# Bias rows and norm vectors of a graph network: operands filled up with zeros to 128 rows and columns

## The chip, the cores and the metric

The kernel runs on one core of one Trainium2 chip. The metric is the device time of one execution in microseconds (us). Names of the engines in the views: PE is TensorE's matmul, PEld its weight load, DVE is VectorE, ACT is ScalarE, POOL is GpSimd, SP is SyncE, which here only issues transfers. A matmul's stationary operand is called its weights; "granted clock" is the share of TensorE's full clock.

## The reference

There are 32 independent batches of a graph with 512 nodes, 128 features each, and an adjacency matrix of zeros and ones. Four graph layers follow each other, each on relu(layernorm(x)) and with a residual addition. All four are needed to place the change; the change itself is in the second (layer 1):

```python
x = x + max over neighbours of relu(p_i + q_j + b)          # layer 0
x = x + L1(relu(layernorm(x)), adj)                         # layer 1
x = x + (adj / rowsum(adj)) @ (h @ weight) + bias           # layer 2
x = x + four GRU steps with messages adj.T @ (h @ W)        # layer 3

# L1: four inner layers; nodes are the concatenated earlier outputs
src_agg = l2norm(adj, rows)      @ (nodes @ ws + bs)
dst_agg = l2norm(adj, columns).T @ (nodes @ wd + bd)
out     = tanh(concat(src_agg, nodes @ wn + bn, dst_agg) @ wu + bu)
```

The bias of the aggregated terms, bs and bd, reaches a node weighted by the sum of its normalised adjacency row or column. With zeros and ones this sum is the square root of the degree.

## The kernel before

**Weights.** `FastWeights` prepares what all batches share. Its constructor makes an identity, index codes and other constants directly, before the planner runs. `rest` folds ws, wn and wd of layer 1 with wu into the weights `w1`, and folds bs and bd with wu into eight rows per inner layer: `b8`, a tile of [8, 4, 128] in fp32r (a form of f32 that TensorE reads in one pass). Eight rows are needed because the weights and the degree vectors are each kept in a high and a low part for precision.

**One batch** goes through `prepare`, `gathers`, `layer1` and `layer23`.

- `prepare` loads x and the adjacency, forms the first layernorm (xn), the transposed adjacency (at, through pat) and the degrees (deg). Then it forms six vectors of norms, `sc`, a tile of [128, 6, 4] f32: GpSimd takes the power -1/2 of the degrees (two vectors), multiplies by the degree (g), rounds that to fp32r (g1, copied into sc) and subtracts (the last write into sc). `dinv` is the square of the first vector. One transposition on TensorE, `psc`, turns the 24 columns of sc into 24 rows, ScalarE copies them (sct), and SP writes them to a table in device memory, `scals`. The key matmuls (pkey) and the maximum over them (top, row, idx) stand around this in time.
- `gathers` computes layer 0: indirect transfers (G) bring most neighbours' rows, one-hot matmuls (pa, from oh and qhl) the others, and VectorE takes the maximum (gm, acc).
- `layer1` reads the table back, once as broadcast scales (rbc) and twice as rows (row8, 8 rows of 512). ScalarE rounds row8 into `rows`, [8, 512] fp32r. For each of the four inner layers it aggregates (pg, from hi and lo against at and an), and forms the output in one accumulator, `pu`: first the bias rows' matmul of b8 and rows, 8 rows high, and then the f32 matmuls with w1 over the features (hT, f) and aggregates (ag). A tanh on ScalarE makes f.
- `layer23` does layers 2 and 3 (pg, po, ph, pk, phn, pxn, gates, zc, nn, h).

An f32 matmul over 512 columns is recorded as two instructions, an fp32r one as one.

**The order of the work** is not written out. `Flow` is a planner in the kernel: operations are noted with an estimated cost (`cost`, `mm`, `tr`), their dependencies follow from tiles and regions, and a list scheduler (`step`) issues them engine by engine, by due times with hand-set leads (`LEADS`). Up to six parts are open at a time, so parts of several batches interleave on every engine. A matmul's cost is taken from its moving columns and type alone, not from its rows. Where the planner foresees TensorE idle, it puts in `spin` matmuls without use (line 534). Nearly all operations carry the line of the planner's call, L510, so the views are read by tile names.

Buffers: tiles with a `tag` come from rings of `bufs` places; `rows` has one place, `sc` four.

```python
self.note("pe", self.nc.tensor.matmul, (out, lhsT, rhs), {"start": start, "stop": stop},
          [group or out], [lhsT, rhs], cost, 0.16)
```

Of the kernel before, what the change touches and what calls it, by code (L numbers as in the profile page):

```python
# [13 lines left out]
F32 = mybir.dt.float32  # L14
F32R = mybir.dt.float32r
# [4 lines left out]
ALU = mybir.AluOpType  # L20
# [4 lines left out]
P = 128  # L25
# [35 lines left out]
NL1 = 4  # L61
# [4 lines left out]
def flat(t):  # L66
    return t.rearrange("p t d -> p (t d)")
# [217 lines left out]
class Flow:  # L285
# [46 lines left out]
    def fixed(self, t, shape, dtype):  # L332

        return View(Buf(None, 0, shape[0], t), shape, dtype)
# [269 lines left out]
class FastWeights:  # L604
# [5 lines left out]
    def __init__(self, nc, F, a, const, mid, ps):  # L610
        self.F, self.mid, self.ps = F, mid, ps
        self.NL3 = a["L3_gnn_weight"].shape[0]
        n = a["x"].shape[1]

        def fixed(shape, dtype, name):
            return const.tile(shape, dtype, name=name)

        ident = fixed([P, P], F32, "ident")
        make_identity(nc, ident)
        identb = fixed([P, P], BF16, "identb")  # L620
        nc.vector.tensor_copy(identb, ident)
        self.ident, self.identb = ident, identb
        self.mhalf = fixed([P, 8], F32, "mhalf")
        nc.gpsimd.memset(self.mhalf, -0.5)

        self.ones = fixed([P, P], F32, "ones")
        nc.gpsimd.memset(self.ones, 1.0)  # L630
        ltf = fixed([P, P], F32, "ltf")
        nc.gpsimd.affine_select(
            ltf, self.ones, pattern=[[1, P]], compare_op=ALU.is_ge, fill=0.0, base=0,
            channel_multiplier=-1,
        )
        nc.gpsimd.memset(ltf[0:HP, HP:P], 0.0)
        self.lt = fixed([P, P], F32R, "lt")
        nc.vector.scalar_tensor_tensor(self.lt, ident, NBASE, ltf, ALU.mult, ALU.add)
        self.ltk = fixed([P, P], BF16, "ltk")
        nc.vector.tensor_scalar(self.ltk, self.lt.bitcast(F32), KEY, None, ALU.mult)  # L640
        self.code = fixed([P, n // P, P], BF16, "code")
        icode, code = fixed([P, n // P], I32, "icode"), fixed([P, n // P], F32, "fcode")
        for t, (first, step) in enumerate(CODES):
            nc.gpsimd.iota(
                icode[:, t : t + 1], pattern=[[1, 1]], base=first, channel_multiplier=step
            )
        nc.vector.tensor_copy(code, icode)
        for t in range(n // P):
            nc.vector.tensor_scalar(
                self.code[:, t, :], ident, code[:, t : t + 1], None, ALU.mult  # L650
            )


        self.sign = fixed([P, 2], F32, "sign")
        nc.gpsimd.memset(self.sign[:, 0:1], -1.0)
        nc.gpsimd.memset(self.sign[:, 1:2], 1.0)
        nc.gpsimd.memset(self.sign[0:4, 0:1], 1.0)
        nc.gpsimd.memset(self.sign[0:4, 1:2], 0.0)
        self.nc, self.a, self.const, self.n = nc, a, const, n

    def own(self, shape, dtype, name):
        return self.F.tile(self.const, shape, dtype, name, name)

    def temp(self, tag, name, wide=False):
        shape = [P, 2, self.n] if wide else [P, 4, P]
# [26 lines left out]
    def rest(self):  # L692

        F, a, ident, NL3 = self.F, self.a, self.ident, self.NL3

        n3 = 3 * NL3
        brow = self.temp("zc", "brow")[:, 0, :]
        F.pool.memset(brow, 0.0)
        rows = [
            ((nm, i), a[f"L1_gnn_{nm}{i}"].unsqueeze(0), 1)  # L700
            for i in range(NL1) for nm in ("bs", "bd", "bn", "bu")
        ] + [
            (nm, a[f"L3_gnn_b_{nm}"].rearrange("l (g c) -> (l g) c", c=P), n3)
            for nm in ("ih", "hh")
        ]
        col, at = {}, 0
        for key, src, m in rows:
            col[key] = at
            (F.sync, F.act)[len(col) % 2].dma_start(out=brow[at : at + m, :], in_=src)
            at += m  # L710
        pb = self.psum("pb")
        F.tr(pb[:, 0, :], brow, ident)
        bcol = self.own([P, P], F32, "bcol")
        F.vec.tensor_copy(bcol, pb[:, 0, :])
        self.bih = bcol[:, col["ih"] : col["ih"] + n3]
        self.bhh = bcol[:, col["hh"] : col["hh"] + n3]
        self.bsum = self.own([P, n3], F32, "bsum")
        F.vec.tensor_add(self.bsum, self.bih, self.bhh)

        self.w1, self.bu = [], self.own([P, NL1], F32, "bu")

        self.b8 = self.own([8, NL1, P], F32R, "b8r")
        bm = self.own([P, NL1, 2, 8], F32, "bm")
        F.pool.memset(bm, 0.0)
        for i in range(NL1):
            for k, nm in enumerate(("bs", "bd")):
                c = col[nm, i]
                F.act.copy(bm[:, i, k, k::2], bcol[:, c : c + 1].to_broadcast([P, 4]))  # L730
        for i in range(NL1):
            ch = NCH[i]
            wu = self.temp("x2", f"wu{i}")[:, 0:3, :]
            F.sync.dma_start(out=wu, in_=a[f"L1_gnn_wu{i}"].rearrange("(c p) v -> p c v", p=P))
            w1 = self.own([P, 3, ch, P], F32, f"w1_{i}")
            for k, nm in enumerate(("ws", "wn", "wd")):
                w = self.temp(("f", "hg", "hT1")[k], f"{nm}{i}")[:, 0:ch, :]
                (F.sync, F.act)[k % 2].dma_start(
                    out=w, in_=a[f"L1_gnn_{nm}{i}"].rearrange("(c p) v -> p c v", p=P)
                )  # L740
                pt = self.psum(f"pwt_{i}_{k}")
                for c in range(ch):
                    F.tr(pt[:, c, :], w[:, c, :], ident)
                wt = self.temp(("gate0", "xn2")[k % 2], f"wt_{i}_{k}")[:, 0:ch, :]
                F.vec.tensor_copy(wt, pt[:, 0:ch, :])
                pw = self.psum(f"pw_{i}_{k}")
                for c in range(ch):
                    F.mm(pw[:, c, :], wt[:, c, :], wu[:, k, :], start=True, stop=True)
                F.act.copy(w1[:, k, :, :], pw[:, 0:ch, :])
            self.w1.append(w1)  # L750
            pv = self.psum(f"pv_{i}")
            c = col["bn", i]
            F.mm(
                pv[:, 2, 0:1], wu[:, 1, :], bcol[:, c : c + 1], start=True, stop=True, group=pv
            )
            for k in range(2):
                F.mm(
                    pv[0:8, 0, :], bm[:, i, k, :], wu[:, 2 * k, :],
                    start=(k == 0), stop=(k == 1), group=pv,
                )  # L760
            c = col["bu", i]
            F.vec.tensor_add(self.bu[:, i : i + 1], bcol[:, c : c + 1], pv[:, 2, 0:1])
            hi = F.tile(self.mid, [P, 4, P], F32R, "hi1", f"bhi_{i}", 1)[0:8, 0, :]
            F.act.copy(hi, pv[0:8, 0, :])
            full = self.temp("nn", f"bfull_{i}")[0:8, 0, :]
            F.vec.tensor_scalar(full, pv[0:8, 0, :], self.sign[0:8, 1:2], None, ALU.mult)
            F.vec.scalar_tensor_tensor(
                self.b8[:, i, :], hi.bitcast(F32), self.sign[0:8, 0:1], full, ALU.mult, ALU.add
            )

    def last(self):
# [51 lines left out]
def fast(ctx: ExitStack, tc: tile.TileContext, a: dict, out: bass.AP, bad):  # L823
    nc = tc.nc
    x, adj, nodemask = a["x"], a["adj"], a["nodemask"]
    B, N, D = x.shape
    assert D == P and N % P == 0
    NT = N // P

    const = ctx.enter_context(tc.tile_pool(name="const", bufs=1))  # L830
    small = ctx.enter_context(tc.tile_pool(name="small", bufs=3))
# [3 lines left out]
    F = Flow(nc, PACE, AHEAD)  # L835
# [9 lines left out]
    mid = ctx.enter_context(tc.tile_pool(name="mid", bufs=1))  # L845
    W = FastWeights(nc, F, a, const, mid, ps)
# [6 lines left out]
    for i in range(2):  # L853
        t = dram.tile([ROWS, P], F32, name=f"qtab{i}")
        k = (ROWS - 2 * P) // P
# [75 lines left out]
    def prepare(b, xt, af):  # L931
# [83 lines left out]

        dm = F.tile(small, [P, 2, NT], F32, tag="dm", name=f"dm_{b}", bufs=4)
        F.pool.tensor_scalar(dm, deg, 1.0, None, ALU.max)
        sc = F.tile(small, [P, 6, NT], F32, tag="sc", name=f"sc_{b}", bufs=4)
        F.pool.tensor_tensor(
            sc[:, 0:2, :], dm, W.mhalf[:, 0 : 2 * NT].rearrange("p (k t) -> p k t", k=2), ALU.pow  # L1020
        )
# [30 lines left out]
        F.vec.tensor_scalar(idx, row[:, :, 0:NLEFT], ROWS - 1, None, ALU.bitwise_and)  # L1052

        pt = pst(0, f"psc_{b}")
        F.tr(pt[0 : 6 * NT, 0, :], sc.rearrange("p k t -> p (k t)"), W.ident)
        sct = F.tile(small, [6 * NT, P], F32, tag="sct", name=f"sct_{b}", bufs=1)
        F.act.copy(sct, pt[0 : 6 * NT, 0, :])
        F.sync.dma_start(out=scals[b % 2].rearrange("k (t p) -> (k t) p", p=P), in_=sct)
# [49 lines left out]
    def layer1(b, x1, an, at, dinv):  # L1108
# [3 lines left out]
            F.sync.dma_start(out=row8[4 * h : 4 * h + 4, :], in_=scal[2:6, :])  # L1112
        rbc = F.tile(mid, [P, 2, N], F32, tag="rbc", name=f"rbc_{b}")
        F.sync.dma_start(out=rbc, in_=scal[0:2, :].unsqueeze(0).to_broadcast([P, 2, N]))
        rows = F.tile(mid, [8, N], F32R, tag="rows", name=f"rows_{b}")

        xn = norm(1, x1, f"{b}_1")
        two = sbuf_parts(1, xn, f"{b}_1")
        F.act.copy(rows, row8)
        pt = transposed(1, xn, f"pt_{b}_1")  # L1120
        hT = F.tile(mid, [P, NT, P], F32, tag="hT1", name=f"hT_{b}_1")
        F.act.copy(hT, pt)
# [3 lines left out]
        for i in range(NL1):  # L1126
# [10 lines left out]
                F.vec.tensor_mul(ag[:, k, :], flat(pg), rbc[:, k, :])  # L1137
            agg[new] = ag
            pu = pst(1, f"pu_{b}_{i}")
            F.mm(flat(pu), W.b8[:, i, :], rows, start=True, stop=False)  # L1140
            late = []
            for c, nm in enumerate(names):
                F.mm(flat(pu), w[:, 1, c, :], flat(feat[nm]), start=False, stop=False)
# [626 lines left out]
```

## Time and profile before

| | |
|---|---|
| median of 3 runs | 2941.53 us (2940.82 to 2942.3) |
| profiled execution | 2943.54 us, span 2941.8 us |
| mean granted TensorE clock | 0.993 |
| busy, TensorE matmul | 2843.4 us (97% of the span), 11493 records |
| busy, VectorE | 2384.2 us (81%) |
| busy, GpSimd | 1827.3 us (62%) |
| busy, ScalarE | 1218.1 us (41%) |
| bias rows' matmuls | 128 |
| transpositions psc | 32 |

The span runs from the first to the last instruction of one profiled execution; its own time is a little longer. Busy times are unions of an engine's instructions. Matmuls are pipelined, so their records overlap, and the rate of TensorE is read from the distances between their starts.

A matmul's form in the views reads rows*columns of the weights, then partitions x elements of what is written or read: "8*128 8x512" is a matmul with 8 rows of weights, 128 columns, and 512 moving columns; "128*24 128x128" is the transposition of 24 columns. "x4" in a timeline means four records in a row.

### The profile page before, as it was taken

What the parts mean: (1) busy time and instruction counts of PE and PEld (TensorE: products, weight loads), DVE (VectorE), ACT (ScalarE), POOL (GpSimd) and SP (SyncE); (2) the same over time, 40 slices, a digit from 0 to 9 for tenths busy, and PEclk for the clock granted to TensorE, in tenths of its full rate; (3) what the DMA queues carried; (4) which work ended last, traced back from release to release, by engine and by line L of the source; (5) the groups of instructions that cost most, each with busy time, mean ns of one, the idle gap of its engine ahead of it and who ended that gap; (6) DMA issues with size and microseconds to landing.
All of it is one profiled execution on the core that took longest, in us unless ns stands there. A gap on an engine that the chain in (4) does not pass through costs nothing.

```text
span 2941.8 us, 37748 instructions
## 1 busy us (share of the span) xinstructions
PE 2843.4 (97%) x11493; PEld 1753.8 (60%) x11513; DVE 2384.2 (81%) x5382; ACT 1218.1 (41%) x2547; POOL 1827.3 (62%) x2013
## 2 busy tenths in 40 slices
PE   7899999999999999999999999999999999999997
PEld 3555556666666566666666566666666666555555
DVE  6988878888888898888888888889888888887533
ACT  2434434434444344344444444444344444333323
POOL 4676667666666666666666666666666666565312
PEclk8999999999999999999999999999999999999999
DMA  7642434334334334333433433343333333342100
GB/s 154 145 91 48 84 69 86 85 72 81 65 66 86 85 74 86 59 72 80 86 85 73 84 61 65 86 87 77 80 68 69 75 86 84 56 77 37 33 4 9
DMA packets 191267, 218.44 MB, mean 74 GB/s; under 512 B 30376, under 2 KB 139600, under 8 KB 191056
## 3 DMA queue, kind: packets, MB, share of 16 engines
q0 software_dynamic: 47104, 92.34, 22.2%
q1 hardware_dynamic: 73768, 63.63, 7.4%
q10 hardware_dynamic: 70184, 59.98, 6.7%
q8 instruction: 93, 1.52, 0.2%
q14 instruction: 118, 0.97, 0.1%
HBM read 164.32 MB, written 17.96 MB: 62 GB/s over the span
## 4 chain that ended last, share of the span: by engine, by line
PE 80%; DVE 10%; issue 4%; DMA 2%; ACT 2%; POOL 1%; ACTq 0%; SPq 0%; DVEq 0%; POOLq 0%
PE pg L510 25%; PE pu L510 19%; PE pk L510 15%; PE pa L510 6%; PE phn L510 4%; PE pxn L510 3%; DVE acc L510 3%; PE pkey L510 2%; PE ph L510 2%; PE pf L510 2%; PE po L510 1%; DMA G<-qtab,idx 1%; DVE nn L510 1%; PE pt L510 1%; DVE x L510 1%
## 5 line engine op out<-in xcount | busy, mean ns | idle before, releaser
L510 POOL DMA_INDIRECT G<-qtab,idx x768 | 848.6, 1105 | 589.6 <-DVE gm L510 453.3
L510 DVE TENSOR_TENSOR acc<-acc,pa 128x512 f32<-128x512 f32 x992 | 673.6, 679 | 146.4 <-PE pa L510 134.5
L510 PE MATMUL pa<-oh,qhl 128*128 128x512 f32 x1024 | 465.7, 510 | 11.2 <-DVE oh L510 5.3
L510 PE MATMUL pg<-an,hi 128*128 128x512 f32 (+1 forms) x1040 | 457.3, 441 | 0.6 <-DVE acc L510 0.4
L510 PE MATMUL pu<-ag,w 128*128 128x512 f32 x896 | 448.0, 592 | 0.5 <-DVE ag L510 0.3
L510 PE MATMUL pg<-an,lo 128*128 128x512 f32 (+1 forms) x1040 | 436.0, 422 | 0.0
L510 DVE TENSOR_SCALAR oh<-ccd 128x1024 fp32r<-128x1024 bf16 x512 | 393.9, 787 | 13.3 <-PE pa L510 13.2
L510 PE MATMUL pg<-at,lo 128*128 128x512 f32 x640 | 295.9, 462 | 0.8 <-DVE lo L510 0.4
L510 PE MATMUL pg<-at,hi 128*128 128x512 f32 x640 | 281.1, 439 | 7.2 <-DVE acc L510 1.8
L510 PEld LDWEIGHTS pa<-oh,qhl 128*128 128x128 f32 x1024 | 193.9, 191 | 152.2 <-issue 40.4
L510 ACT ACTIVATE xn<-x,shift,rstd 128x128 f32<-128x128 f32 x512 | 211.5, 484 | 171.6 <-POOL shift L510 170.1
L510 DVE TENSOR_TENSOR gm<-gm,G 128x128 f32<-128x128 f32 x768 | 253.4, 331 | 8.7 <-DMA G<-qtab,idx 7.7
L510 PE MATMUL pk<-h,g_hh 128*128 128x512 f32 (+1 forms) x528 | 256.3, 590 | 0.6 <-DVE top L510 0.6
L510 PEld LDWEIGHTS pg<-an,hi 128*128 128x128 f32 x1040 | 195.1, 188 | 93.2 <-issue 49.1
L510 PEld LDWEIGHTS pg<-an,lo 128*128 128x128 f32 x1040 | 195.2, 188 | 84.7 <-issue 40.3
L510 PE MATMUL pk<-mT,g_ih 128*128 128x512 f32 (+1 forms) x528 | 242.3, 580 | 1.4 <-ACT mT L510 1.1
L510 ACT ACTIVATE gate<-pk,bsum 128x512 f32<-128x512 f32 (+1 forms) x264 | 176.9, 673 | 140.8 <-PE pk L510 137.3
L510 PEld LDWEIGHTS pu<-ag,w 128*128 128x128 f32 x896 | 168.1, 189 | 110.9 <-issue 80.0
L510 POOL TENSOR_TENSOR rstd<-rstd,mhalf 128x4 f32<-128x4 f32 x128 | 139.8, 1092 | 138.8 <-DVE shift L510 133.6
L510 DVE TENSOR_TENSOR ag<-pg,rbc 128x512 f32<-128x512 f32 x256 | 174.8, 684 | 61.3 <-PE pg L510 58.5
L510 ACT COPY mT<-pg 128x512 f32<-128x512 f32 (+1 forms) x164 | 94.2, 575 | 304.6 <-PE pg L510 300.0
L510 ACT CAST hi<-ph 128x512 fp32r<-128x512 f32 (+1 forms) x99 | 56.8, 574 | 341.2 <-PE ph L510 333.4
(172 smaller groups left out, 5110.4 us busy)
## 6 DMA issues: line engine op xcount, KB each, us to landing
af<-in_adj_dram ACTq DMA_DIRECT2D x32, 1024.0 KB
ccd<-cc SPq DMA_DIRECT2D x512, 64.0 KB
an<-in_adj_dram POOLq DMA_DIRECT2D x128, 256.0 KB, 3.9
x<-in_x_dram ACTq DMA_DIRECT2D x64, 256.0 KB
rbc<-scal SPq DMA_DIRECT2D x32, 512.0 KB
G<-qtab,idx POOLq DMA_INDIRECT x768, 3.8
qtab<-qn SPq DMA_DIRECT2D x128, 64.0 KB
out_dram<-xo ACTq DMA_DIRECT2D x32, 256.0 KB
```

The source lines that it names most:

```text
L510: op.fn(*(real(v) for v in op.args), **{k: real(v) for k, v in op.kw.items()})
```

## The change

The bias rows `b8` and the degree rows `rows` become tiles of 128 partitions, zero in all but the first eight, and the matmul reads all 128. `rows` is now one fixed tile, written anew in rows 0 to 7 for each batch. The norm vectors are views of the first 24 columns of a [128, 128] tile, of which there are two, `vectors`, taken in turn by batches; the columns behind are zero, and psc transposes all 128 columns. What is copied out of psc stays 24 rows. The zeros are written once, at the start: fp32r tiles by VectorE as the identity times 0.0 (`zeros`), the vectors by GpSimd.

```diff
@@ FastWeights.__init__
         self.nc, self.a, self.const, self.n = nc, a, const, n
+        self.rows = self.zeros([P, n // P, P], "rows")
+        self.vectors = []
+        for i in range(2):
+            t = fixed([P, P], F32, f"vectors{i}")
+            nc.gpsimd.memset(t, 0.0)
+            self.vectors.append(F.fixed(t, [P, P], F32))
+    def zeros(self, shape, name):
+        t = self.const.tile(shape, F32R, name=name)
+        for k in range(shape[1]):
+            self.nc.vector.tensor_scalar(t[:, k, :], self.ident, 0.0, None, ALU.mult)
+        return self.F.fixed(t, shape, F32R)
@@ FastWeights.rest
-        self.b8 = self.own([8, NL1, P], F32R, "b8r")
+        self.b8 = self.zeros([P, NL1, P], "b8r")
...
-                self.b8[:, i, :], hi.bitcast(F32), self.sign[0:8, 0:1], full, ALU.mult, ALU.add
+                self.b8[0:8, i, :], hi.bitcast(F32), self.sign[0:8, 0:1], full, ALU.mult, ALU.add
@@ prepare
-        sc = F.tile(small, [P, 6, NT], F32, tag="sc", name=f"sc_{b}", bufs=4)
+        full = W.vectors[b % 2]
+        sc = full[:, 0 : 6 * NT].rearrange("p (k t) -> p k t", t=NT)
...
-        F.tr(pt[0 : 6 * NT, 0, :], sc.rearrange("p k t -> p (k t)"), W.ident)
+        F.tr(pt[:, 0, :], full, W.ident)
@@ layer1
-        rows = F.tile(mid, [8, N], F32R, tag="rows", name=f"rows_{b}")
...
-        F.act.copy(rows, row8)
+        F.act.copy(flat(W.rows[0:8]), row8)
...
-            F.mm(flat(pu), W.b8[:, i, :], rows, start=True, stop=False)
+            F.mm(flat(pu), W.b8[:, i, :], flat(W.rows), start=True, stop=False)
```

## Prediction

> **What bounds the kernel now.** I read the page first: the busy shares, the slices and the chain that ended last.
>
> ```profile
> span 2941.8 us, 37748 instructions
> ...
> PE 2843.4 (97%) x11493; PEld 1753.8 (60%) x11513; DVE 2384.2 (81%) x5382; ACT 1218.1 (41%) x2547; POOL 1827.3 (62%) x2013
> ...
> PE   7899999999999999999999999999999999999997
> ...
> PE 80%; DVE 10%; issue 4%; DMA 2%; ACT 2%; POOL 1%; ACTq 0%; SPq 0%; DVEq 0%; POOLq 0%
> ```
>
> TensorE is busy 97% of the span, in every slice but the first two and the last, and it makes up 80% of the chain; VectorE is the only other name of weight there. A busy share says nothing of whether the matmuls run at their best rate, so I then took the windows view, of five batches in the middle and of the stretch in which VectorE is fullest.
>
> ```profile
> core 0: us, PE busy (x) PEld busy (x) DVE busy (x) ACT busy (x) POOL busy (x), PEclk, DMA share, GB/s
> 919.00:1379.00 460.00, 454.96 (x1849) 282.53 (x1849) 387.80 (x878) 199.01 (x414) 306.05 (x336) 1.00 0.37 76
> 1486.75:1506.19 19.44, 19.39 (x61) 10.39 (x59) 18.92 (x30) 6.97 (x16) 12.51 (x14) 1.00 0.44 103
> ```
>
> In the middle TensorE idles 5 us of 460, at full clock; VectorE has 16% free, but in the second window only 0.52 us of 19.44. One batch lasts 86.57 us there (two transpositions psc start at 1445.05 and 1531.62). So in the middle a us of TensorE time is a us of the kernel, unless VectorE is in the way.
>
> The rows that change are few. By tile, the bias rows' matmul:
>
> ```profile
> L510 PEld LDWEIGHTS pu<-rows,b8r x128: 181/182/183, 131.6 to 2842.4; 8*128 8x128 f32 x128
> L510 PE MATMUL pu<-rows,b8r x128: 462/490/638, 131.6 to 2842.4; 8*128 8x512 f32 x128
> ```
>
> 128 of them, 8 rows high, and 32 psc with 24 columns. Durations are of no use, as matmuls overlap; the price is in the distance from start to start. The timeline of TensorE around one bias matmul (start, duration, x how many):
>
> ```profile
> 1487.07 0.39 PE L510 MATMUL pg<-an,lo 128*128 128x512 f32 x1
> 1487.30 0.39 PE L510 MATMUL pa<-oh,qhl 128*128 128x512 f32 x1
> 1487.62 0.49 PE L510 MATMUL pu<-rows,b8r 8*128 8x512 f32 x1
> 1488.04 1.98 PE L510 MATMUL pu<-f,w 128*128 128x512 f32 x4
> 1489.86 1.02 PE L510 MATMUL pu<-ag,w 128*128 128x512 f32 x2
> 1490.72 0.60 PE L510 MATMUL ph<-ident,h 128*128 128x128 f32 x4
> ...
> 1492.87 1.02 PE L510 MATMUL pk<-h,g_hh 128*128 128x512 f32 x2
> 1493.33 0.80 PE L510 MATMUL pg<-an,hi 128*128 128x512 f32 x1
> ```
>
> Two fp32r matmuls of 128 rows are 0.23 us apart (1487.07 to 1487.30). The bias matmul starts 0.32 after the one before it, and the next one 0.42 after it. An f32 matmul is two records of 0.43 (1489.86 to 1490.72 is 0.86); the four after the bias matmul take 1.82 where 1.72 is due. And around one psc:
>
> ```profile
> 1530.21 0.28 PE L510 MATMUL pt<-ident,xn 128*128 128x128 f32 x1
> 1530.32 0.22 PE L510 MATMUL pkey<-code,at 128*128 128x128 bf16 x1
> ...
> 1531.56 0.22 PE L510 MATMUL pkey<-code,at 128*128 128x128 bf16 x1
> 1531.62 0.27 PE L510 MATMUL psc<-ident,sc 128*24 128x128 f32 x1
> 1531.84 1.98 PE L510 MATMUL pk<-h,g_hh 128*128 128x512 f32 x4
> 1533.26 0.79 PE L510 MATMUL pg<-an,hi 128*128 128x512 f32 x1
> ```
>
> A transposition with 128 columns is followed after 0.11 us (pt at 1530.21), psc after 0.22; and from pk to pg are 1.42, where three records and the first start after f32 (0.03, from 1492.87 to 1493.33 less one record) make 1.32. No wait is reported at any of these.
>
> **What the Trainium skill says.** TensorEngine Tiling (Array Packing), section Key Properties: changing the tiling mode, not just the tile, drains TensorE. The trace agrees in kind: every matmul of fewer rows or columns is dear on entry, on leaving, and once more after it; that a drain is the cause it does not show. TensorE: Matmul & The Clock Gate, section LDWEIGHTS, says that the load's time goes by columns, not rows; here 182 ns for 8 rows and 189 for 128 agree. The same page's closing table gives a single matmul of 32 rows the time of one with 128; in this stream that does not hold, since it costs the distances above.
>
> **The change, part by part.**
>
> 1. Bias matmul with 128 rows (b8, rows). It becomes an fp32r matmul like pa or pg beside it, 0.23 us apart. Saved: 0.32 - 0.23 = 0.09 before it, 0.42 - 0.23 = 0.19 after it, 1.82 - 1.72 = 0.10 at the one after. The other common surrounding, at 1524.17, gives 0.33, 0.42, 0.34: 0.40. I take 0.38, times 128 = 48.6 us. Bounds: 0 (the distances belong to something other than the shape) and 0.40 x 128 = 51.
>
> 2. psc with 128 columns (vectors). Saved 0.11 + 0.10 = 0.21, times 32 = 6.7 us. Its weight load grows from 93 ns to that of other f32 transpositions (140); that lies beside the pkey matmuls, and pt above stands in the same place at the ordinary distance. Bounds 0 and 7.
>
> 3. Zero fills at the start: 8 VectorE multiplications of 128x128 (rows 4, b8r 4), 0.2 us apart by the code<-ident row (three in 0.67): 1.6 us; two GpSimd memsets of 0.2. In the new order they stand ahead of wsq, which now starts at 4.40, when its weights land. From ident's end at 1.52, all that stands ahead is about 2.9 us: wsq some 0.1 late. VectorE then sits idle for 10.71 us and GpSimd for 18.22, so nothing; without that cover, 2 us.
>
> 4. Order and waits. Queue by queue the two programs' orders differ on SP nowhere, on TensorE, VectorE and ScalarE only in batches 1 to 6 (some 470 TensorE places of 12750, about 110 us), with 7 spin matmuls fewer; spins fill idle time and are worth nothing. Bounds +6 and -6 us: TensorE idles 3.3 us (276 to 368) and 5.8 us (368 to 460) there. I take 0. On GpSimd each batch has one swap: the next batch's rstd (1.01 us) now comes ahead of the subtraction that finishes sc, and dinv goes behind both. The subtraction, done at 1530.15 now, would be done near 1531.1, and behind it wait shift, dinv and lo. psc starts at 1531.62, so 0.5 us stay, and TensorE, gm on VectorE and gm on GpSimd come earlier together. Taken as 0, bound +0.2 us a batch (6 us). shift gets no later, as rstd goes earlier by the two small operations (0.3 us). Semaphore waits at the bias matmul and at psc stay the same, and the DMAs too. ACT still copies 8 rows (620 ns); W.rows stays one buffer, so that copy waits for the same readers.
>
> Gross: 48.6 + 6.7 = 55.3 us, 1.73 a batch. **What of it counts.** Batches in the middle (from 460 to 2481, 22 of 32, with idle of about 1% of TensorE): 38 us. There one bias matmul of four lies in VectorE's full stretch (1487.62). VectorE idles there 0.17 (for a gate, from pk) and 0.25 (for pxn), both for TensorE's work, which comes 0.38 earlier: it can follow, with nothing to spare. I count 95%: 36 us. The other 10 batches' 17.3 us lie where TensorE idles more (23.6 and 10.8 us in the first two batch lengths, waiting for loads; 2.5 to 17 in the last five); I count 0.6: 10.4. Sum 46.5. The profiled execution took 2943.5 (span 2941.8 and 1.7 around it), 2.0 over the median of 2941.5: 2943.5 - 46.5 - 2.0 = 2895; I say 2894.
>
> **Rivals.**
>
> A. VectorE takes over (0.22). For it: 18.92 us busy of 19.44. Then the saving of that bias matmul is lost in each batch (12 us), and with it half of the ends: 55.3 - 12 - 9 = 34, 2907. Were two of four lost, 2919. Against it: its waits there are for TensorE.
>
> B. The distances are not of the shape but of the change of accumulators or of new operands (0.05): 2941. Against it: pa and pg with 128 rows change bank just as often at 0.23, and psc shows the same with another operand type.
>
> C. Slower (0.03): psc waits for GpSimd. The subtraction now stands behind rstd, and rstd waits for VectorE's rstd, ready at about 1529.58, 0.2 us before its turn. If VectorE comes later by x, psc, and all of TensorE behind it, comes later by x - 0.5 in each batch. It turns the sign when x is over 2.2 us (0.5 + 1.73); at 3 us the kernel is at 2941.5 + 32 x 0.77 = 2966. Against it: VectorE's own work before rstd hangs on TensorE, which is earlier.
>
> **How the numbers follow.** Full effect 0.70 (2882 to 2902, likeliest 2894); A 0.22 (2902 to 2919); B 0.05; C 0.03. Bottom: all 55.3 and 4 from a better order, 2882. Top: 2918, within A. A measurement of this kernel tells about 0.2% (6 us) from no change: faster 0.92, same 0.05, slower 0.03.
>
> **What would show it.** In the changed profile the bias matmul reads 128*128 and stands 0.23 from both neighbours; what follows psc comes 0.11 after it; psc to psc in the middle is 84.9 us in place of 86.57; TensorE stays at 97% busy or near. For A: TensorE waits for h or acc of VectorE by 0.3 us or more in each batch, and the period is near 85.3. For C: psc has a wait for sc on GpSimd. I am wrong in the main step if the distances stay at 0.32 and 0.42.

## The result and the profile after

The changed kernel takes 2911.86 us (2909.39 to 2913.61, 4 runs) against 2941.18 us of the kernel before (4 runs): ratio 0.9902, 95% interval 0.9885 to 0.9919. It is faster by 29 us, 1.0%. The profiled execution took 2913.61 us, its span is 2911.8. The forecast was 2894 with a range of 2882 to 2918: right in direction, and the time lies in the range, but the gain is 29 us where 47 were forecast.

From the page of the changed kernel, busy shares and the chain that ended last:

```profile
PE 2804.0 (96%) x11506; PEld 1759.5 (60%) x11506; DVE 2387.9 (82%) x5390; ACT 1218.0 (42%) x2547; POOL 1829.6 (63%) x2015
...
PE 71%; POOL 10%; issue 8%; DVE 7%; DMA 2%; ACT 2%; ACTq 0%; POOLq 0%; SPq 0%; DVEq 0%
```

TensorE's busy time fell by 39 us, more than the kernel's. In the chain TensorE went from 80% to 71%, and GpSimd from 1% to 10%: a new name in the chain is the first sign of where a gain stops.

**The bias rows.** The timeline of TensorE around one of them (start, duration, x how many):

```profile
1496.20 0.40 PE L510 MATMUL pa<-oh,qhl 128*128 128x512 f32 x1
1496.44 0.40 PE L510 MATMUL pu<-rows,b8r 128*128 128x512 f32 x1
1496.68 1.02 PE L510 MATMUL pu<-hT,w 128*128 128x512 f32 x2
1497.53 1.02 PE L510 MATMUL pu<-ag,w 128*128 128x512 f32 x2
```

0.24 before it, 0.24 after it, and 0.85 for the two records that follow: the distances 0.32, 0.42 and the extra 0.10 are gone. At each of the four places of a batch, TensorE is 0.38 or 0.39 us shorter as the median of the middle batches, as forecast.

**psc.** The same view, and the weight loads' timeline (PEld) of the kernel before at the same place:

```profile
1514.91 0.28 PE L510 MATMUL psc<-ident,vectors 128*128 128x128 f32 x1
1515.14 1.98 PE L510 MATMUL pk<-h,g_hh 128*128 128x512 f32 x4
1516.56 0.79 PE L510 MATMUL pg<-an,hi 128*128 128x512 f32 x1
```

```profile
1531.56 0.09 PEld L510 LDWEIGHTS psc<-ident,sc 128*24 128x24 f32 x1
1531.84 0.30 PEld L510 LDWEIGHTS pk<-h,g_hh 128*128 128x128 f32 x2 [0.18 <-ACT h L510]
```

With 128 columns pk still comes 0.23 after psc, and pg 1.42 after pk. The weight load of pk had been waiting for ScalarE's copy h all along. ScalarE's timeline of the kernel before has it from 1531.20 for 0.59:

```profile
1531.20 0.59 ACT L510 COPY h<-pt 128x512 f32<-128x512 f32 x1 [0.28 <-PE pt L510]
```

It ends at 1531.79, and pk's weights load 0.05 us later; in the changed kernel h ends at 1515.09, and pk starts at 1515.14.

**The batch.** The distance from one psc to the next (below: the period), as the median of 20 in the middle (the 9th to the 28th of 31), is 85.75 us, against 86.56. So 0.81 of 1.73 us a batch arrived. In 22 middle batches that is 18.8 us in all (36 were forecast), and 11.2 at the two ends (10.4 forecast). The next table lays one batch of the middle out between events of the two traces, in us; "hi" and "lo" are layer 2's. The bias matmuls are counted from the one ahead of VectorE's full stretch.

| | before | after | saved | bias matmuls inside |
|---|---|---|---|---|
| psc to the bias matmul ahead of VectorE's full stretch | 42.58 | 42.07 | 0.51 | fourth |
| from there to VectorE's h | 18.48 | 18.59 | -0.11 | first |
| h to hi on ScalarE | 9.78 | 9.79 | -0.01 | second |
| hi to the next psc | 15.72 | 15.30 | 0.42 | third |

The first and the second bias matmul lie in the two stretches that did not get shorter. TensorE has less to do there, and waits instead. At the end of the first of these stretches, in the kernel before and in the changed one:

```profile
1505.45 0.69 DVE L510 TENSOR_TENSOR h<-gate,nn 128x512 f32<-128x512 f32 x1
1506.19 0.66 PE L510 MATMUL ph<-ident,h 128*128 128x128 f32 x4
```

```profile
1489.17 0.68 DVE L510 TENSOR_TENSOR h<-gate,nn 128x512 f32<-128x512 f32 x1
1489.90 0.66 PE L510 MATMUL ph<-ident,h 128*128 128x128 f32 x4 [0.29 <-DVE h L510]
```

In both, ph starts 0.05 us behind the end of h. The kernel before reports no wait there, and yet TensorE had no slack: a saving just ahead could only become a wait. The same holds at lo of layer 2: the pg that reads it starts 0.05 behind its end in both kernels. From the view of TensorE's waits in the changed kernel (us in total, times, longest):

```profile
PE ph L510 <- DVE h L510: 12.7, 29, 2.1
...
PE pg L510 <- POOL lo L510: 7.4, 24, 0.7
```

Before, the wait for h was 7.3 us in 11 times, and that for lo 0.2 us, once.

### The profile page after: what moved, and what is told of

The parts are those of the page before. It is cut to its first block, busy times and chain, and to the rows that moved or that the text cites. A ratio compares the mean times of both kernels' runs of the same rounds, so it can differ in the third digit from the quotient of the medians.

```text
span 2911.8 us, 37760 instructions
## 1 busy us (share of the span) xinstructions
PE 2804.0 (96%) x11506; PEld 1759.5 (60%) x11506; DVE 2387.9 (82%) x5390; ACT 1218.0 (42%) x2547; POOL 1829.6 (63%) x2015
## 3 DMA queue, kind: packets, MB, share of 16 engines
q8 instruction: 93, 1.52, 0.2%
## 4 chain that ended last, share of the span: by engine, by line
PE 71%; POOL 10%; issue 8%; DVE 7%; DMA 2%; ACT 2%; ACTq 0%; POOLq 0%; SPq 0%; DVEq 0%
PE pg L510 22%; PE pk L510 14%; PE pu L510 14%; PE pa L510 5%; POOL G L510 5%; PE phn L510 3%; PE pxn L510 3%; DVE acc L510 2%; PE ph L510 2%; PE pkey L510 1%; PE po L510 1%; POOL rstd L510 1%; POOL lo L510 1%; DVE nn L510 1%; DMA G<-qtab,idx 1%
## 5 line engine op out<-in xcount | busy, mean ns | idle before, releaser
L510 PE MATMUL pg<-an,hi 128*128 128x512 f32 (+1 forms) x1040 | 450.6, 435 | 0.5 <-DVE acc L510 0.4
L510 DVE TENSOR_TENSOR gm<-gm,G 128x128 f32<-128x128 f32 x768 | 260.9, 340 | 9.7 <-DMA G<-qtab,idx 8.0
```

Of the source, the lines that this page charges most:

```text
L510: op.fn(*(real(v) for v in op.args), **{k: real(v) for k, v in op.kw.items()})
```

## Experiments

Each ratio is taken against the kernel before, run beside it on the same chip.

**1 to 3: which part, and how many places count.** The first undoes the psc part, the second does it alone, the third leaves out the bias rows' matmul itself and so takes more away at the same places.

```diff
 # e1_bias_only (from the changed kernel; the tiles `vectors` go too)
...
-        full = W.vectors[b % 2]
-        sc = full[:, 0 : 6 * NT].rearrange("p (k t) -> p k t", t=NT)
+        sc = F.tile(small, [P, 6, NT], F32, tag="sc", name=f"sc_{b}", bufs=4)
...
-        F.tr(pt[:, 0, :], full, W.ident)
+        F.tr(pt[0 : 6 * NT, 0, :], sc.rearrange("p k t -> p (k t)"), W.ident)
```

> Bias rows padded, psc and its vectors as before; every engine's order is then that of the kernel before. Theory (waits elsewhere take two of the four bias matmuls' savings in a batch, and padding psc is worth nothing, as pk behind it waits for ScalarE's copy h): about 2911 us, the same as with both, period from psc to psc in the middle 85.8 us. Rival 1 (the saving was lost to the new order and the swapped rstd on GpSimd): about 2895, period 85.0. Rival 2 (psc carried a part of the 29 us): about 2918, period 86.0.

Measured: 2915.29 us, ratio 0.9907 (0.9890 to 0.9924), period 85.76. The bias rows alone carry the whole gain. But for the zero fills at the start, the order of all engines was that of the kernel before, so the loss is not one of order.

```diff
 # e2_psc_only (from the kernel before; the tiles `vectors` are made as in the change)
...
-        sc = F.tile(small, [P, 6, NT], F32, tag="sc", name=f"sc_{b}", bufs=4)
+        full = W.vectors[b % 2]
+        sc = full[:, 0 : 6 * NT].rearrange("p (k t) -> p k t", t=NT)
...
-        F.tr(pt[0 : 6 * NT, 0, :], sc.rearrange("p k t -> p (k t)"), W.ident)
+        F.tr(pt[:, 0, :], full, W.ident)
```

> psc padded, with its vectors, bias rows 8 high as before; every engine's order is that of the changed kernel. Theory: 2941 us, no change from before, distance from psc to pk stays 0.22, period 86.6. Rival 1 (the new order costs): slower than before by 10 to 18 us, 2951 to 2959, period 87.0. Rival 2 (psc carries 7 us): 2934, period 86.35.

Measured: 2940.11 us, ratio 0.9995 (0.9986 to 1.0003), period 86.52. Psc's columns and the order that came with its tiles together move the time by no more than the interval leaves, 4 us down to 1 us up; the 6.7 us forecast for psc lie outside it.

```diff
 # e3_no_bias (from the changed kernel)
             F.mm(flat(pu), W.b8[:, i, :], flat(W.rows), start=True, stop=False)
+            F.part[-1].fn = lambda *args, **kw: None
...
-                F.mm(flat(pu), w[:, 1, c, :], flat(feat[nm]), start=False, stop=False)
+                F.mm(flat(pu), w[:, 1, c, :], flat(feat[nm]), start=(c == 0), stop=False)
```

> The changed kernel without the bias rows' matmul: it keeps its place in the plan but is not issued, so the bias of the aggregated terms is left out of layer 1; all orders stay. It takes away another 4 x 0.23 us of TensorE per batch at the same four places. Theory (two of the four places lie beside a path through VectorE and GpSimd that sets the time): half counts, 0.46 us a batch, about 2898 us, period 85.3. Rival (all four places count, the loss was elsewhere): 0.92 a batch, about 2883, period 84.85.

Measured: 2897.95 us, ratio 0.9849 (0.9832 to 0.9865), period 85.27: 0.48 of the 0.92 us taken away. Of a second saving at the same four places, too, about half arrives.

**4 and 5: is the first one lost to VectorE's full stretch?** VectorE gets less to do inside it, in both kernels: its check of the adjacency values (`junk`) reads a part of them. The planner still counts the whole operation, so that no order changes.

```diff
             junk, af2, 1.0, af2, ALU.is_equal, ALU.not_equal, accum_out=bad[:, b : b + 1]
         )
+        few = slice(0, N // 2)
+        F.part[-1].args = (
+            junk[:, few], af2[:, few], 1.0, af2[:, few], ALU.is_equal, ALU.not_equal
+        )
```

> The changed kernel with VectorE's check of the adjacency values (junk) over a quarter of the values, some 1.5 us less on VectorE per batch inside its full stretch ahead of h; all orders stay. It leaves out three quarters of that check. Theory (the first lost bias saving waits for h, which VectorE's full stretch sets): TensorE's wait for h in the middle (0.29 idle) goes, period 85.75 to about 85.3, time about 2900 us. Rival (only GpSimd, or latencies alone, hold it there): period 85.7, time 2911.

What stays is 256 of the 2048 values that the check reads in each partition, an eighth and not a quarter, in this run and in all others that shorten the check: it takes 0.41 us in place of 2.28, so 1.87 us less and not 1.5.

Measured: 2897.13 us, ratio 0.9850 (0.9834 to 0.9867), period 85.45. The view of TensorE's waits in this run:

```profile
PE ph L510 <- DVE h L510: 6.6, 8, 2.1
```

From 29 waits for h to 8: the wait in the middle is gone, and with it 0.30 us a batch. In 22 batches that is about 7 us of the 15 that this run is ahead of the changed kernel; most of the rest came at the start, where the first psc is 2.1 us earlier and the first five distances are 8.7 shorter in sum. That the total hit is in part luck: a period of 85.3 was expected.

Why do 1.87 us less on VectorE bring only 0.30? The timelines of VectorE and GpSimd in the changed kernel, ahead of the h that ends at 1489.85:

```profile
1479.39 2.28 DVE L510 SCALAR_TENSOR_TENSOR junk<-af 128x2048 bf16<-128x2048 f32 x1
1480.98 1.60 POOL L510 DMA_INDIRECT G<-qtab,idx  x1 [0.30 <-issue]
...
1485.20 1.85 DVE L510 TENSOR_TENSOR gm<-gm,G 128x128 f32<-128x128 f32 x1
1485.62 1.28 POOL L510 TENSOR_TENSOR gate<-h,gate 128x512 f32<-128x512 f32 x1
```

and at the same place in the kernel before:

```profile
1501.74 1.60 DVE L510 TENSOR_TENSOR gm<-gm,G 128x128 f32<-128x128 f32 x1
1501.88 1.30 POOL L510 TENSOR_TENSOR gate<-h,gate 128x512 f32<-128x512 f32 x1
```

GpSimd's gather issue (G) ends 0.91 us behind VectorE's check, in 20 of the 21 middle batches of either kernel; GpSimd's gate comes behind it; and VectorE's gm, which takes 0.28 in most places, lasts until 0.16 behind gate's end, in 19 of 21. So the path to h leads from the check over GpSimd back to VectorE. With `junk` shortened, the issue takes 1.03 us, gate ends 0.31 us earlier behind the bias matmul (15.33 in place of 15.64, medians), and h with it (18.28 in place of 18.59). VectorE then idles 0.53 and 1.19 us inside the stretch: behind the check, its amount of work is not what h waits for.

> The kernel before with the same cut of the check. Theory: its wait for h is 0.2 us, so at most that: period 86.35, about 2936 us, and the difference to the changed kernel with the same cut grows from 29 to about 36 us. Rival: no change, 2941.

Measured: 2932.24 us, ratio 0.9975 (0.9964 to 0.9987), period 86.50. The middle gained 0.06 here (gate ends 0.04 us earlier behind the bias matmul); the rest of the 9 us is at the start, where the first psc comes 1.9 us earlier and the first five distances are shorter in sum. With the check shortened in both, the change is worth 35 us and 1.05 a batch, where it was 0.81.

**6 and 7: is the second one lost to layer 2's layernorm?** From h on, TensorE waits for what the layernorm makes, hi and lo. GpSimd's timeline in the changed kernel, behind that h (ended 1489.85):

```profile
1493.88 1.10 POOL L510 TENSOR_TENSOR rstd<-rstd,mhalf 128x4 f32<-128x4 f32 x1 [2.90 <-DVE shift L510]
1495.17 1.88 POOL L510 DMA_INDIRECT G<-qtab,idx  x1 [0.19 <-issue]
1497.08 0.22 POOL L510 TENSOR_TENSOR shift<-shift,rstd 128x4 f32<-128x4 f32 x1
1497.45 1.33 POOL L510 DMA_INDIRECT G<-qtab,idx  x1 [0.15 <-DVE ag L510]
1499.08 0.94 POOL L510 DMA_INDIRECT G<-qtab,idx  x1 [0.31 <-issue]
1500.04 1.29 POOL L510 TENSOR_TENSOR lo<-xn,hi 128x512 fp32r<-128x512 f32 x1
```

and on TensorE, where it ends:

```profile
1501.39 0.50 PE L510 MATMUL pg<-at,lo 128*128 128x512 f32 x1 [0.29 <-POOL lo L510]
```

Gather issues (G) stand between rstd and shift, and ahead of lo. Experiments 6 and 7 hold them back when the operations are issued, without a change in the plan. `gather` picks these issues out, `mark` is set on layer 2's rstd, shift and lo, and `flush` issues what was held:

```diff
...
+    def emit(self, op):
+        mark = getattr(op, "mark", None)
+        gather = op.engine == "pool" and op.after > 2.0 and any(isinstance(v, Rows) for v in op.kw.values())
+        if gather and self.mark in ("rstd", "shift"):
+            self.held = [*self.held, op]
+            return
+        if any(u in self.held for u in op.before):
+            self.flush()
+        op.fn(*(real(v) for v in op.args), **{k: real(v) for k, v in op.kw.items()})
+        if mark:
+            self.mark = mark
+            if mark in ("shift", "lo"):
+                self.flush()
...
```

> The changed kernel with another order on GpSimd alone: in layer 2's layernorm of each batch, shift goes ahead of the gather issue that stood before it, and lo ahead of the two after it; all other orders stay. Theory (the second lost bias saving waits for hi and lo of this layernorm, 9.8 us behind h): hi comes 1.9 us earlier and lo 1.5, the waits of pg for them go, period about 85.1, time about 2893 us. Rival (gathers delayed by up to 2 us make VectorE late, or the layernorm is not the path): no gain, 2911 or more.

Measured: 2914.91 us, ratio 0.9909 (0.9893 to 0.9926), period 86.03. That is no gain, and a miss. The lines of GpSimd, VectorE and TensorE in this run, from the timeline, say why:

```profile
1246.49 1.29 POOL L537 TENSOR_TENSOR x<-x,b 128x512 f32<-128x512 f32 x1
...
1246.66 1.27 DVE L537 TENSOR_TENSOR gm<-gm,G 128x128 f32<-128x128 f32 x1
...
1250.43 0.49 PE L537 MATMUL po<-w,mT 128*128 128x128 f32 x2 [1.37 <-DVE x L537]
```

hi and lo came earlier by 1.4 and 1.5 us behind h, and the waits of pg for lo went from 24 to 2. But GpSimd's addition x then ran beside VectorE's gm, which took 1.27 us in place of 0.28. TensorE came to po 0.6 us earlier behind h, VectorE's x 0.3 us later, and po waited 1.37 us for it in place of 0.51. The Trainium skill gives a reason, in SBUF - State Buffer, section "SBUF: two separate sides": VectorE operations with two SBUF inputs and GpSimd operations that read SBUF take one pair of ports in turn, as an exclusive lock. The trace agrees with that: gm ended 0.15 us behind GpSimd's x.

> The kernel before with the same order on GpSimd. Theory: its waits there are 0.2 us each, so period about 86.2, time about 2931 us, and the difference to the changed kernel with that order grows to about 38 us. Rival: 2941.

Measured: 2947.43 us, ratio 1.0018 (1.0011 to 1.0025), period 86.84. A miss too: the same collision (po waits 1.01 us, as the median), with less to gain.

**8 to 11: the same without the collision.** x (marked x2) now goes ahead of the held gathers too:

```diff
# against experiments 6 and 7
-        if gather and self.mark in ("rstd", "shift"):
+        if gather and self.mark in ("rstd", "shift", "lo"):
-            if mark in ("shift", "lo"):
+            if mark in ("shift", "x2"):
                 self.flush()
...
```

> As the run with another order on GpSimd, from the changed kernel, but x (the bias addition of layer 2) also goes ahead of the two gather issues, right behind lo, so that it no longer runs beside VectorE's gm. Theory (there it was that collision that took the gain back: gm took 1.27 us in place of 0.28, and po waited 1.37 for x in place of 0.51): po's wait goes back to about 0.5, and of the 0.57 us by which TensorE reached po earlier all stays: period about 85.2, time about 2896 us. Rival (delayed gathers, or the layernorm is not the path): period 85.75 or more, 2911 or more.

Measured: 2990.09 us, ratio 1.0150 (1.0135 to 1.0165): slower by far, and period 85.19, as expected. Both are true. In the middle po's wait is back at 0.5 and the gain is there. The sixth distance is 101.9 us where it was 85.8, and the last 92.1 in place of 77.2. From the waits of the stretch from 100 to 700 us:

```profile
DVE gm L537 <- DMA G<-qtab,idx: 56.7, 25, 5.9
```

In the changed kernel VectorE's wait for gathers in that stretch is 1.1 us, once. The reading is that lo comes much later there than the gathers that are held for it; it was not traced gather by gather, but experiment 12 agrees.

> The kernel before with that order on GpSimd. Theory: what it waits at this layernorm is 0.2 to 0.25 us a batch, so period about 86.3, about 2935 us, and the difference to the changed kernel with the same order is about 39 us in place of 29. Rival: the same gain as in the changed kernel (the order helps both alike), 2926.

Measured: 3019.38 us, ratio 1.0251 (1.0235 to 1.0267), period 86.37: the same loss at the ends, and 0.19 gained in the middle.

> The changed kernel with both reliefs: three quarters of the check junk left out, and the GpSimd order with x ahead of the gathers. Theory: both lost bias savings come back, period 84.9, about 2883 us. Rival (the two waits are one, behind each other): no better than the better of the two alone, 2896.

Measured: 2969.91 us, ratio 1.0091 (1.0073 to 1.0108), period 84.88.

> The kernel before with both reliefs (three quarters of the check left out). Theory: period 86.25, about 2928 us, so that the change is worth about 45 us there, near the 48.6 of the bias matmuls. Rival (something else takes a part): the change is worth 29 to 35 us there too.

Measured: 3004.09 us, ratio 1.0197 (1.0180 to 1.0214), period 86.31. The totals of these four miss, as the ends spoil them; the periods hit within 0.1. The middle periods of the eight kernels:

| | before | changed | worth a batch |
|---|---|---|---|
| as they are | 86.56 | 85.75 | 0.81 |
| check shortened | 86.50 | 85.45 | 1.05 |
| layernorm relieved | 86.37 | 85.19 | 1.18 |
| both | 86.31 | 84.88 | 1.43 |

The two reliefs add up: 0.81 + 0.24 + 0.37 = 1.42. With both, the change is worth 1.43 of the 1.52 us that four bias matmuls of 0.38 make. Means over the same 20 distances, which count the few longer batches in, give 0.90, 1.13, 1.24 and 1.42: the same end, and steps of 0.23 and 0.34.

**12: the order where it helps.** In batches 5 to 26 alone, with nothing left out:

> The changed kernel, complete, with shift, lo and x ahead of the gather issues on GpSimd, in batches 5 to 26 alone. In the run that had this in all batches the middle took 85.19 a batch, and the first seven distances from psc to psc and the last lost some 90 us. Theory (the order is right in the middle and wrong at the ends, where the gathers held back for lo are awaited by gm): 22 batches x 0.56 us less than the changed kernel, 2912 - 12 = about 2900 us. Rival (the loss sits in the held gathers themselves and moves to batch 5): 2911 or more.

Measured: 2904.32 us, ratio 0.9853 (0.9836 to 0.9869), period 85.19; the first six distances and the last are within 1.5 us of those of the changed kernel again. This beats both kernels: its interval ends where that of the changed kernel, 0.9885 to 0.9919, has not begun.

## Why the prediction was right, and where it was wrong

The direction and the price of a bias matmul were right; what of it counts was not. That the stated range holds the time is owed to rival A: the full effect alone was given 2882 to 2902.

- **Bias matmuls, 0.38 us each on TensorE: right.** All three distances went as read. That the shape and not a change of accumulators costs them (rival B, no gain) is settled by experiment 1. Why a matmul of 8 rows costs this, no run shows; the comparison with a single matmul of 32 rows goes beyond these runs, which have 8 and 128 rows in a stream.
- **psc, 6.7 us: wrong, worth nothing.** The failed step is "A transposition with 128 columns is followed after 0.11 us ..., psc after 0.22". The distance was read right and put down to the wrong cause. I wrote that no wait was reported; it was reported at the weight load, on PEld (0.18 for ACT h), and the reading went by the matmuls' lines alone. Seven of the 32 psc of the kernel before, in other places, were followed after 0.11 to 0.14 us with their 24 columns: a comparison at hand that would have shown it. With the reading falls the remark that fewer columns are dear as fewer rows are.
- **What of it counts in the middle, 95%: wrong.** 0.81 of 1.73 is 47%. The term read 36 us, and 18.8 arrived. Of the 0.92 a batch that are missing, psc makes 0.21, the stretch with VectorE's check 0.24 and the layernorm 0.37 by the reliefs, together 0.82; the remaining 0.1 stays open.
- **"It can follow, with nothing to spare": wrong.** VectorE's waits in the full stretch were counted as slack (0.17 and 0.25 us). The first went. The second, for pxn, stayed at 0.25, and VectorE did come through it a little earlier: TensorE starts pxn 11.71 us behind the bias matmul in place of 11.86, and VectorE its nn at 12.77 in place of 12.92. But gm behind it lasts until GpSimd's gate has ended, which comes 15.64 us behind the bias matmul in place of 15.53, and h ends 0.11 later. The step left GpSimd out of the path.
- **The ends, 10.4 us: right** in size (11.2), in part by luck: 2.1 of the 17.3 us gross were psc's, which brought nothing.
- **Rival A** (VectorE takes over, 2907 to 2919, given 0.22) came nearest to the number. It named one of the two places, though there the path leads over GpSimd too. Its sign came true by half: the wait for h is 0.27 us a batch as the median, near the 0.3 that it gave, and the period is 85.75, not 85.3. The other place, the 9.8 us of latency from h over VectorE, GpSimd and ScalarE to hi, with a bias matmul beside it, was in no rival.
- **Rival C** (psc waits for GpSimd): not seen in the middle. The subtraction ended at 1514.41, 0.5 us ahead of psc, the margin that was worked out.

## What to carry to other kernels

An engine that is busy 99% of the time is not for that reason the bound of every stretch: look for stretches whose length another chain sets (from one result that the engine waits for to the next), and count a saving inside such a stretch as a longer wait until shown otherwise. A matmul that starts 0.05 us behind the end of its operand, batch after batch, marks the end of such a stretch, even where no wait is reported. A full engine in it need not be what sets it: follow back what released the last operation, and see whether operations on two engines end together. Before a distance between two matmuls is put down to the first one's shape, read what the second one's weight load waited for, and look for the same shape before another neighbour. An issue order that is right in the steady part may be wrong at the start and the end; measure the period and the ends apart.

## What the hardware showed that I had not expected

- In this stream, a matmul with 8 rows of weights cost 0.38 us more of TensorE's time than one with 128. A transposition with 24 columns cost nothing more than one with 128: where nothing else waits, the next matmul starts after 0.11 to 0.14 us (seven of the kernel before), and after 0.11 to 0.17 with 128 columns (seven of the changed one).
- VectorE's gm over 128x128 took 1.27 us beside a GpSimd addition of 1.29 in experiment 6, and 0.28 alone. Beside GpSimd's gate it took 1.60 before the change and 1.85 after it, and ended 0.16 behind gate in both.
- A gather issue on GpSimd took 1.60 us beside VectorE's check in the changed kernel, 1.34 in the kernel before, and 1.03 with the check shortened. With the whole check it ended 0.91 us behind it in both kernels. Why it does so, no run shows.
